# Writing the starting values of two accumulations into the PSUM banks from ScalarE and VectorE, in a kernel of attention and a gated scan

## The chip, the core and the metric

The kernel runs on one core of a Trainium2 chip. A core has five engines with their own instruction queues, each worked in order: PE (TensorE, matrix products, which write only to the accumulator memory PSUM), DVE (VectorE), ACT (ScalarE), POOL (GpSimd) and SP (SyncE, used here to issue DMAs). The scan divides PSUM into 8 banks of 128 partitions by 512 numbers, 2 for y and 6 for all the rest. Weights are loaded into PE by separate instructions (PEld), which overlap products. The metric is the device time of one execution in microseconds (us); lower is better.

## The reference

Two blocks follow each other on x of 8 sequences of 1024 tokens of width 512, each added to x. Everything is float32. The first is a modulated attention with 16 heads; the change does not touch it. The second is a gated state-space scan of inner width 1024 with 16 states:

```
xr, gate = jnp.split(x @ W_in.T, 2, axis=-1)
xr = xr + t_emb[:, None, :]                  # t_emb: the condition, one row per sequence
xc = silu(causal_conv4(xr) + b_conv)
xn = layernorm(xc) * ln_g + ln_b
Bm, Cm, dt = jnp.split(xn @ W_xproj.T, 3, axis=-1)
Ad, Bd = 1.0 + tanh_dt(dt) * A, Bm * minimum(norm(xn), 1.0)
for every token:  h = clip(h * Ad + Bd * xn, -10.0, 10.0);   y_t = sum over states of C * h
y = y + D * xn
return y * silu(gate) @ W_out.T
```

Two sums matter here: the condition added to x @ W_in.T, and D * xn added to y.

## The kernel before

The attention takes the first 3.3 ms, the scan the rest. The scan goes through the 1024 tokens one step at a time, all 8 sequences at once: the state h has 128 partitions (8 sequences x 16 states) by 1024 channels, and a step is one DVE instruction, `step` (L906 to L914, 1.34 us). Before it, `weigh` (L883, ACT) scales the input of that step, which a DMA (`fetch`, L869) has spread over the 128 partitions four steps at a time. After four steps, `products` (L888, PE) multiplies the four states by the masked weights C and adds them in PSUM to y: 8 products of 32 weight columns by 512, which the trace shows as 16 rows. A tile y holds 16 steps; its two banks are one buffer (`ps_y`, L552), so y of the next 16 steps can only begin when the old one has been read.

Around the steps, a chunk of 32 tokens is prepared for the next chunk and finished for the last. The order is written by hand: `at(n, f, ...)` puts a piece of work after step n (L917 to L1003), and every engine gets its instructions in that order. Since all chunks are alike, I give positions 0 to 31 in the repeating chunk: position k is the step k and the pieces placed after it, so `p0 + 51` is position 19. I call the step at position k h(k), and y0 to y7 the eight groups of products of a chunk; group yg is placed at position 4g+4 (y7 at position 0 of the next chunk) and needs h(4g) to h(4g+3).

The pieces that matter:

- `conv_mm` (L638, PE, 8 per chunk, every second position from 21 to 3): four products of x with W_in into a bank, then a fifth (L645) that adds the condition by a product of a 128 x 128 matrix `cond` with repeated columns of the identity. I call them c0 to c7. `conv_in` (ACT) reads the bank, `conv_taps` (DVE) makes the convolution, `conv_out` (ACT) the silu.
- `flip_mm` (L679, PE) turns xs to tokens by channels, `stats`, `center`, `deviation` and `scale` (DVE and ACT) normalise it, `spill` (SP) writes it to DRAM for the fetches, `p_mm` (L670, PE) and `lengths`, `params`, `params_mm`, `params_out`, `spread`, `decay` make the scan's coefficients.
- `fan_mm` (L852, PE) and `fan_out` (L861, ACT, 8 copies of 128 x 512) spread the first four steps of a chunk without a DMA.
- `skip` (L726, DVE) multiplies xt, the normalised tile, by D in place; `add_y` (L807, DVE) adds y from PSUM to it; `gate_y` (L810, DVE) multiplies by the gate. Then `out_flip`, `out_copy`, `out_mm` (PE and ACT) multiply by W_out. `gate_mm` (L792, PE) makes the gate.

Waits that set the order between the engines: h has 6 buffers (`hp`, L547), so h(k) overwrites h(k-6) and waits until the products that read h(k-6) are through: h(2) waits for y7, h(18) for y3. The first group of a tile, y0 or y4, waits until `add_y` has read the tile before. All other banks come from one pool of 6 (`ps_m`, L553).

Of the kernel before, what the change touches and what calls it, by code (L numbers as in the profile page):

```python
# [8 lines left out]
F32 = mybir.dt.float32  # L9
# [6 lines left out]
P = 128  # L16
B = 8
H = 512
KH = H // P
# [503 lines left out]
def gated_scan(ctx, tc, const, tok, x1_d, S, win, tables, w_conv, b_conv, ln_g, ln_b, b_dt, a_log,  # L523
# [44 lines left out]
    x1_now = load_chunk(0)  # L568
    cond_sb = load(cond, "cond", [P, P])
    cw = load(w_conv.rearrange("(k p) j -> p k j", p=P), "cw", [P, KI, 4])  # L570
# [15 lines left out]
    xs_all = tok.tile([P, KI, CW], F32, tag="xq", name="xs")  # L586
    o_sb = tok.tile([P, H], F32, tag="sr", name="o_sb")

    eps = wp.tile([P, 1], F32, name="eps_i")
# [39 lines left out]
    last = {"p": None, "h": None}  # L629

    def load_x1(st, c):
        st["x1"] = load_chunk(c)

    def begin(st):
        nc.scalar.copy(xr[:, :, :, 0:3], xr[:, :, :, TC:])
        st["xs"] = xs_all

    def conv_mm(st, k):  # L638
        ps = st["in", k] = ps_m.tile([P, CW], F32, tag="mm", name="in_ps")
        for kk in range(KH):  # L640
            nc.tensor.matmul(  # L641
                ps, win[kk][:, k * P : (k + 1) * P], st["x1"][:, kk].rearrange("p b t -> p (b t)"),
                start=(kk == 0), stop=False,
            )
        nc.tensor.matmul(  # L645
            ps, cond_sb, ident[:, k * B : (k + 1) * B].unsqueeze(2).to_broadcast([P, B, TC]),
            start=False, stop=True,
        )

# [20 lines left out]
    def p_mm(st):  # L670
        ps = st["pt_ps"] = ps_m.tile([P, NT, P], F32, tag="mm", name="pt_ps")
        for i in range(NT):
            for k in range(KI):
                nc.tensor.matmul(
                    ps[:, i, 0:NX], tile_cols(st["xs"][:, k], i), wx_all[:, k * NX : (k + 1) * NX],
                    start=(k == 0), stop=(k == KI - 1), skip_group_check=True,
                )

    def flip_mm(st, i, half):  # L679
        ps = st["x", i, half] = ps_m.tile([P, 4, P], F32, tag="mm", name="x_ps")  # L680
        for j in range(4):
            nc.tensor.transpose(ps[:, j, :], tile_cols(st["xs"][:, 4 * half + j], i), ident)

# [42 lines left out]
    def skip(st, i):  # L726
        nc.vector.tensor_mul(st["xt", i], st["xt", i], d_bc)

# [14 lines left out]
    def params_mm(st, i):  # L743
        ps = st["xp", i] = ps_m.tile([P, 3, P], F32, tag="mm", name="xp_ps")
        for n in range(3):
            nc.tensor.transpose(ps[:, n], pts[i][:, n * NS : n * NS + P], ident)

# [58 lines left out]

    def add_y(st, i):  # L807
        nc.vector.tensor_add(st["xt", i], st.pop(("y", i)), st["xt", i])  # L808

    def gate_y(st, i):  # L810
        g = st["gate", i]
        nc.vector.tensor_mul(g, st["xt", i], g)

    def out_flip(st, i, half):
        ps = st["gt", i, half] = ps_m.tile([P, 4, P], F32, tag="mm", name="gt_ps")
        for j in range(4):
            k = 4 * half + j
            nc.tensor.transpose(ps[:, j, :], st["gate", i][:, k * P : (k + 1) * P], ident)

# [41 lines left out]
    def fan_out(st, c, half, rs):  # L861
        if half == 0 and rs[0] == 0:
            st["xb"] = xbp.tile([P, 4, DI], F32, name="xb")
            for r in range(4):
                xbs[c * TC + r] = st["xb"][:, r]
        for r in rs:
            nc.scalar.copy(st["xb"][:, r, half * 512 : (half + 1) * 512], st.pop(("fan", r)))  # L867

# [19 lines left out]
    def products(g):  # L888

        c, t = divmod(4 * g, TC)  # L890
        i, q = divmod(t // 4, TT // 4)
        st = sts[c]
        if q == 0:
            st["y", i] = ps_y.tile([P, DI], F32, name="y_ps")
        for hf in range(2):
            for r in range(4):
                nc.tensor.matmul(  # L897
                    st["y", i][32 * r : 32 * r + 32, hf * 512 : (hf + 1) * 512],
                    yws[i][:, 4 * q + r, :],
                    hs[4 * g + r][:, hf * 512 : (hf + 1) * 512],  # L900
                    start=(q == 0), stop=(q == 3), skip_group_check=True,
                )
        for r in range(4):
            del hs[4 * g + r]
# [12 lines left out]
    for c in range(NCH):  # L917
        st, n0 = sts[c], c * TC
        p0 = n0 - TC
        if c > 0:  # L920
            at(p0 + -24 if c > 1 else -34, load_x1, st, c)
        at(p0 + -12, begin, st)
        for k in range(KI):
            at(p0 + -11 + 2 * k, conv_mm, st, k)
            at(p0 + -10 + 2 * k, conv_in, st, k)
            at(p0 + -9 + 2 * k, conv_taps, st, k, (0,))
            at(p0 + -8 + 2 * k, conv_taps, st, k, (1,))
            at(p0 + -7 + 2 * k, conv_taps, st, k, (2,))
            at(p0 + -6 + 2 * k, conv_out, st, k)
        at(p0 + 10, flip_mm, st, 0, 0)  # L930
        at(p0 + 10, flip_mm, st, 0, 1)
        at(p0 + 11, stats, st, 0, 0)
        at(p0 + 11, stats, st, 0, 1)
        at(p0 + 11, center, st, 0)
        at(p0 + 13, deviation, st, 0)
        at(p0 + 14, scale, st, 0)
        at(p0 + 17, spill, st, 0)
        at(p0 + 15, squares, st, 0)
        at(p0 + 27, skip, st, 0)
        at(p0 + 14, flip_mm, st, 1, 0)  # L940
        at(p0 + 14, flip_mm, st, 1, 1)
        at(p0 + 15, stats, st, 1, 0)
        at(p0 + 15, stats, st, 1, 1)
        at(p0 + 15, center, st, 1)
        at(p0 + 16, deviation, st, 1)
        at(p0 + 17, scale, st, 1)
        at(p0 + 24, spill, st, 1)
        at(p0 + 18, squares, st, 1)
        at(p0 + 28, skip, st, 1)
        at(p0 + 21, fan_mm, st, 0)  # L950
        at(p0 + 24, fan_out, st, c, 0, (0, 1))
        at(p0 + 25, fan_out, st, c, 0, (2, 3))
        at(p0 + 26, fan_mm, st, 1)
        at(p0 + 27, fan_out, st, c, 1, (0, 1))
        at(p0 + 28, fan_out, st, c, 1, (2, 3))
        at(p0 + 16, p_mm, st)
        at(p0 + 18, lengths, st)
        at(p0 + 18, params, st, 0)
        at(p0 + 19, params_mm, st, 0)
        at(p0 + 20, params_out, st, 0)  # L960
        at(p0 + 20, params, st, 1)
        at(p0 + 21, params_mm, st, 1)
        at(p0 + 22, params_out, st, 1)
        at(p0 + 22, spread, st)
        at(p0 + 28, decay, st)
        at(p0 + 31, weights, st, 0)
        at(p0 + 46, weights, st, 1)
        at(p0 + 34, order, st, 0)
        at(p0 + 39, gate_mm, st, 0, 0)
        at(p0 + 41, gate, st, 0, 0)  # L970
        at(p0 + 41, gate_mm, st, 0, 1)
        at(p0 + 42, gate, st, 0, 1)
        at(p0 + 51, add_y, st, 0)
        at(p0 + 53, gate_y, st, 0)
        at(p0 + 61, out_flip, st, 0, 0)
        at(p0 + 62, out_copy, st, 0, 0)
        at(p0 + 64, out_mm, st, 0, 0)
        at(p0 + 64, out_flip, st, 0, 1)
        at(p0 + 65, out_copy, st, 0, 1)
        at(p0 + 69, out_mm, st, 0, 1)  # L980
        at(p0 + 71, out_store, st, 0)
        at(p0 + 76, out_send, st, c, 0)
        at(p0 + 49, order, st, 1)
        at(p0 + 50, gate_mm, st, 1, 0)
        at(p0 + 52, gate, st, 1, 0)
        at(p0 + 62, gate_mm, st, 1, 1)
        at(p0 + 67, gate, st, 1, 1)
        at(p0 + 67, add_y, st, 1)
        at(p0 + 72, gate_y, st, 1)
        at(p0 + 75, out_flip, st, 1, 0)  # L990
        at(p0 + 76, out_copy, st, 1, 0)
        at(p0 + 79, out_mm, st, 1, 0)
        at(p0 + 76, out_flip, st, 1, 1)
        at(p0 + 77, out_copy, st, 1, 1)
        at(p0 + 80, out_mm, st, 1, 1)
        at(p0 + 82, out_store, st, 1)
        at(p0 + 90, out_send, st, c, 1)
    for g in range(S // 4):
        if g % (TC // 4) > 0:
            at(4 * g - 9 if g > 2 else -24, fetch, g)  # L1000
        at(4 * g + 4, products, g)
# [14 lines left out]
def network(ctx: ExitStack, tc: tile.TileContext, S, ins, out):  # L1016
# [22 lines left out]
    with tc.manual_schedule():  # L1039
        modulated_attention(  # L1040
            tc, const, xp, tok, x1_d, xu_d, S, ins["x"], ins["xT"], ins["cond"],
            {n: ins[f"w{n}T"] for n in "qkvwu"}, ident, ins["condT"], early, handover,
        )
        gated_scan(
            tc, const, tok, x1_d, S, win, tables, ins["w_conv"], ins["b_conv_c"], ins["ln_g"], ins["ln_b"],
            ins["b_dt"], ins["a_log"], ins["d_skip"], ins["w_out"], ident, ins["cond_k"], ins["mask_y"], ins["sel"], out,
        )
# [70 lines left out]
```

## Time and profile before

| | us |
|---|---|
| median of three runs | 5761.65 (5761.53 to 5765.28) |
| the profiled execution itself | 5764.81 |
| span of its profile | 5763.0 |
| PE busy, of the span | 5582.3 (97%) |
| DVE busy | 4451.3 (77%) |
| ACT busy | 3968.4 (69%) |

The profile comes from one execution. "Busy" is the time in which an engine had an instruction in work; consecutive instructions overlap by some tenths of a microsecond, so the time that one costs in a row of others is the distance from its start to the start of the next, which is less than its duration. "Idle before" is the time that an engine stood still before an instruction, with the engine and line whose end released it; where that line had long been done, it was another. PEclk is the clock that PE was granted, 1.00 being full speed. Lines are those of the kernel before (L...).

The attention ends at about 3338 us. From 3450 us on the scan repeats itself chunk by chunk: y4 starts at 4032.73, 4106.21, 4179.69, 4254.32, 4327.81, 4401.29, 4474.78, 4548.26 us.

### The profile page before, as it was taken

What the parts mean: (1) busy time and instruction counts of PE and PEld (TensorE: products, weight loads), DVE (VectorE), ACT (ScalarE), POOL (GpSimd) and SP (SyncE); (2) the same over time, 40 slices, a digit from 0 to 9 for tenths busy, and PEclk for the clock granted to TensorE, in tenths of its full rate; (3) what the DMA queues carried; (4) which work ended last, traced back from release to release, by engine and by line L of the source; (5) the groups of instructions that cost most, each with busy time, mean ns of one, the idle gap of its engine ahead of it and who ended that gap; (6) DMA issues with size and microseconds to landing.
All of it is one profiled execution on the core that took longest, in us unless ns stands there. A gap on an engine that the chain in (4) does not pass through costs nothing.

```text
span 5763.0 us, 114139 instructions
## 1 busy us (share of the span) xinstructions
PE 5582.3 (97%) x43564; PEld 3242.2 (56%) x43564; DVE 4451.3 (77%) x6930; ACT 3968.4 (69%) x6995; POOL 1541.0 (27%) x1668
## 2 busy tenths in 40 slices
PE   7999999999999999999999989999999999999998
PEld 4656656556556655656566555555555555555553
DVE  4666766766766767667666669999999999999997
ACT  5565655655655655656555568888888888888886
POOL 2433433434434434434333311111111111111111
PEclk9999999999999999999999999999999999999999
DMA  2111212111112112022111268888888888888887
GB/s 83 33 34 54 52 47 62 31 60 51 40 49 67 24 52 72 19 66 55 40 53 31 89 173 230 232 228 229 231 230 228 230 227 230 230 227 229 229 229 189
DMA packets 376962, 714.80 MB, mean 124 GB/s; under 512 B 198176, under 2 KB 280240, under 8 KB 347232
## 3 DMA queue, kind: packets, MB, share of 16 engines
q1 hardware_dynamic: 346416, 684.66, 44.2%
q0 software_dynamic: 30000, 22.83, 1.4%
q8 instruction: 346, 5.67, 0.4%
q14 instruction: 200, 1.64, 0.1%
HBM read 596.58 MB, written 83.89 MB: 118 GB/s over the span
## 4 chain that ended last, share of the span: by engine, by line
PE 62%; DMA 13%; DVE 10%; ACT 9%; SPq 3%; issue 3%; POOL 0%; DVEq 0%; ACTq 0%; POOLq 0%
PE mm_ps L129 17%; PE t_ps L295 14%; PE s_ps L285 9%; DMA xb<-xd 9%; PE t_ps L302 8%; DVE h L910 4%; PE in_ps L641 4%; SPq L876 3%; ACT xb L886 3%; PE y_ps L897 2%; PE o_ps L835 2%; ACT pr L456 2%; PE g_ps L795 1%; DMA bca<-few 1%; DMA x<-x_d 1%
## 5 line engine op out<-in xcount | busy, mean ns | idle before, releaser
L446 DVE TENSOR_REDUCE nmax<-s_ps 128x1 f32<-128x1024 f32 x1024 | 1206.3, 1220 | 460.1 <-PE s_ps L288 459.4
L453 ACT COPY pT<-t_ps 128x512 f32<-128x512 f32 x1024 | 550.7, 589 | 1297.2 <-PE t_ps L295 1296.7
L910 DVE CUSTOM_DVE_ANT_0 h<-h,xb,lim 128x1024 f32<-128x1024 f32 x1024 | 1374.6, 1342 | 81.6 <-ACT x1t L790 26.4
L295 PEld LDWEIGHTS t_ps<-ident,pr 128*128 128x128 f32 x8192 | 911.3, 141 | 659.2 <-issue 490.3
L886 ACT ACTIVATE xb<-xb,ws 128x1024 f32<-128x1024 f32 x1024 | 1157.9, 1163 | 16.9 <-DMA xb<-xd 12.5
L456 ACT ACTIVATE pr<-s_ps,nmax 128x1024 f32<-128x1024 f32 x1024 | 1140.1, 1128 | 1.5 <-DVE nmax L446 1.3
L295 PE MATMUL t_ps<-ident,pr 128*128 128x128 f32 x8192 | 1096.7, 277 | 28.4 <-ACT pT L453 24.7
L475 POOL TENSOR_SCALAR pr<-pr,rinv 128x1024 f32<-128x1024 f32 x512 | 572.5, 1118 | 129.4 <-DVE rinv L474 121.9
L285 PE MATMUL s_ps<-kT,qT 32*128 32x512 f32 x2048 | 596.0, 641 | 2.5 <-ACT pr L456 1.8
L897 PE MATMUL y_ps<-h,yw 128*32 128x512 f32 x4096 | 521.0, 609 | 64.7 <-DVE xt L808 51.7
L288 PE MATMUL s_ps<-k,q 32*128 32x512 f32 x2048 | 578.0, 640 | 1.1 <-DMA q<-qT 1.1
L461 POOL TENSOR_SCALAR pr<-pr,rinv 128x1024 f32<-128x1024 f32 x256 | 286.7, 1120 | 1071.1 <-PE t_ps L295 751.9
L302 PEld LDWEIGHTS t_ps<-pT,vt 128*32 128x32 f32 x16384 | 433.9, 110 | 204.5 <-DVE rinv L469 113.7
L302 PE MATMUL t_ps<-pT,vt 128*32 128x128 f32 x16384 | 506.9, 274 | 16.0 <-DVE pT L467 9.3
L470 POOL TENSOR_SCALAR pr<-pr,rinv 128x1024 f32<-128x1024 f32 x256 | 286.4, 1119 | 841.8 <-DVE rinv L469 792.4
L641 PE MATMUL in_ps<-x,win 128*128 128x256 f32 x2048 | 495.4, 385 | 0.0
L795 PE MATMUL g_ps<-win,x1t 128*128 128x512 f32 x1024 | 467.2, 599 | 1.2 <-ACT x1t L790 1.2
L835 PE MATMUL o_ps<-wout,xt 128*128 128x512 f32 x1024 | 459.0, 596 | 0.0
L641 PEld LDWEIGHTS in_ps<-x,win 128*128 128x128 f32 x2048 | 378.3, 191 | 133.4 <-ACT xb L867 49.4
L847 POOL DMA_DIRECT2D out<-o_sb x256 | 150.9, 595 | 1038.1 <-ACT o_sb L841 965.5
L758 POOL DMA_DIRECT2D bca<-few x256 | 129.1, 513 | 1094.8 <-ACT few L751 1056.3
L467 DVE COPY pT<-t_ps 128x512 f32<-128x512 f32 x512 | 352.0, 688 | 54.3 <-PE t_ps L295 54.1
(149 smaller groups left out, 7181.0 us busy)
## 6 DMA issues: line engine op xcount, KB each, us to landing
xb<-xd SPq DMA_DIRECT2D x1792, 256.0 KB
xd<-xt SPq DMA_DIRECT2D x64, 512.0 KB
q<-qT SPq DMA_DIRECT2D x128, 128.0 KB
xr<-in_xT SPq DMA_DIRECT2D x64, 256.0 KB
xu_d<-xr SPq DMA_DIRECT2D x64, 256.0 KB
xr<-xu_d SPq DMA_DIRECT2D x64, 256.0 KB
x_d<-xr SPq DMA_DIRECT2D x64, 256.0 KB
out<-o_sb POOLq DMA_DIRECT2D x256, 64.0 KB, 5.5
```

What stands on the lines that cost most here:

```text
L129: nc.tensor.matmul(ps, w, x, start=(k == 0), stop=(k == KH - 1))
L285: nc.tensor.matmul(s_ps[i][:, 0:HW], st["q"][r, qc], st["k"][r, 0:HW], start=True, stop=True)
L288: nc.tensor.matmul(s_ps[i][:, HW:S], st["q2"][r, qc], st["k2"][r], start=True, stop=True)
L295: nc.tensor.transpose(ps[:, j], pr[:, c0 : c0 + P], ident)
L302: nc.tensor.matmul(av[r], vt[:, kt, r], pT[:, i, kt], start=(kt == 0), stop=(kt == KT - 1), skip_group_check=True,)
L446: nc.vector.tensor_reduce(nmax[i], s_ps[i], AX.X, ALU.max, negate=True)
L456: nc.scalar.activation(fresh[i], s_ps[i], AF.Exp, bias=nmax[i], accum_out=rsum[i])
L641: nc.tensor.matmul(ps, win[kk][:, k * P : (k + 1) * P], st["x1"][:, kk].rearrange("p b t -> p (b t)"), start=(kk == 0), stop=False,)
L835: nc.tensor.matmul(ps, st["gT", i][:, k, :], wout_sb[:, k, :], start=False, stop=(k == KI - 1), skip_group_check=True,)
L886: nc.scalar.mul(xbs[n], xbs[n], sts[c]["ws"][:, t : t + 1])
L897: nc.tensor.matmul(st["y", i][32 * r : 32 * r + 32, hf * 512 : (hf + 1) * 512], yws[i][:, 4 * q + r, :], hs[4 * g + r][:, hf * 512 : (hf + ...
L910: nc.vector._custom_dve(dve_ops.TENSOR_ADD_SAT, out=h, in0=last["h"], in1=xbs.pop(n), s0=lim[:, 0, t : t + 1], s1=lim[:, 1, t : t + 1],)
```

## The change

1. `conv_mm` loses the fifth product. Two positions earlier a new piece `conv_open` (ACT) writes the condition into the bank by a copy from SBUF to PSUM, and the four products add to it.
2. `skip` takes a y tile and writes D * xn into its two banks (DVE, SBUF to PSUM); all products of that tile add to it. `add_y` is gone, and `gate_y` reads y from PSUM.
3. Of the 8 copies of `fan_out`, 4 go to DVE.
4. At the start of the scan 8 more products write all banks once, with `start` set. Later the flips and `p_mm` set `start` on the first product of a bank only, and the products of `conv_mm` and `products` not at all; `p_mm` gets one more product (128 x 160 zeros) for the columns that its others leave out.
5. Many pieces move by some positions. `skip` goes from positions 27 and 28 to 3 (first tile, right after `gate_y` of the tile before) and 20 (second tile, after `gate_y` at 19 and the step h(20)). The second `params` moves from 20 to 19, `params_mm` of it from 21 to 20, the flips of the first tile from 10 to 9, `gate_mm` of the first tile's second half from 9 to 11, the load of x for the chunk after next from 8 to 15.

```diff
-    cond_sb = load(cond, "cond", [P, P])
+    cT = load(cond.rearrange("(k p) b -> p k b", p=P), "cT", [P, KI, B])
...
+    for _ in range(6):
+        ps = ps_m.tile([P, CW], F32, tag="mm", name="any_ps")
+        nc.tensor.matmul(ps, ident, ident[:, 0:1].to_broadcast([P, CW]), start=True, stop=True)
+    ps = ps_y.tile([P, DI], F32, name="y_ps")
+    for hf in range(2):
+        nc.tensor.matmul(
+            ps[:, hf * 512 : (hf + 1) * 512], ident, ident[:, 0:1].to_broadcast([P, 512]), start=True, stop=True
+        )
...
+    def flip(ps, x, start, stop):
+        nc.tensor.matmul(ps, x, ident, start=start, stop=stop, is_transpose=True, skip_group_check=True)
...
+    def conv_open(st, k):
+        ps = st["in", k] = ps_m.tile([P, CW], F32, tag="mm", name="in_ps")
+        nc.scalar.copy(ps.rearrange("p (b t) -> p b t", b=B), cT[:, k].unsqueeze(2).to_broadcast([P, B, TC]))
+
     def conv_mm(st, k):
-        ps = st["in", k] = ps_m.tile([P, CW], F32, tag="mm", name="in_ps")
+        ps = st["in", k]
         for kk in range(KH):
             nc.tensor.matmul(
                 ps, win[kk][:, k * P : (k + 1) * P], st["x1"][:, kk].rearrange("p b t -> p (b t)"),
-                start=(kk == 0), stop=False,
-            )
-        nc.tensor.matmul(
-            ps, cond_sb, ident[:, k * B : (k + 1) * B].unsqueeze(2).to_broadcast([P, B, TC]),
-            start=False, stop=True,
-        )
+                start=False, stop=(kk == KH - 1), skip_group_check=True,
+            )
...
+        nc.tensor.matmul(
+            ps[:, :, NX:], ident, zero[:, 0:1].unsqueeze(2).to_broadcast([P, NT, P - NX]),
+            start=False, stop=True, skip_group_check=True,
+        )
...
     def skip(st, i):
-        nc.vector.tensor_mul(st["xt", i], st["xt", i], d_bc)
+        y = st["y", i] = ps_y.tile([P, DI], F32, name="y_ps")
+        nc.vector.tensor_mul(y, st["xt", i], d_bc)
...
-    def add_y(st, i):
-        nc.vector.tensor_add(st["xt", i], st.pop(("y", i)), st["xt", i])
-
     def gate_y(st, i):
         g = st["gate", i]
-        nc.vector.tensor_mul(g, st["xt", i], g)
+        nc.vector.tensor_mul(g, st.pop(("y", i)), g)
...
-            nc.scalar.copy(st["xb"][:, r, half * 512 : (half + 1) * 512], st.pop(("fan", r)))
+            (nc.scalar.copy, nc.vector.tensor_copy)[r % 2](st["xb"][:, r, half * 512 : (half + 1) * 512], st.pop(("fan", r)))
...
-        at(p0 + -12, begin, st)
+        at(p0 + -14, begin, st)
         for k in range(KI):
+            at(p0 + -13 + 2 * k, conv_open, st, k)
...
-        at(p0 + 10, flip_mm, st, 0, 0)
-        at(p0 + 10, flip_mm, st, 0, 1)
+        at(p0 + 9, flip_mm, st, 0, 0)
+        at(p0 + 9, flip_mm, st, 0, 1)
...
-        at(p0 + 27, skip, st, 0)
+        at(p0 + 35, skip, st, 0)
...
-        at(p0 + 28, skip, st, 1)
+        at(p0 + 52, skip, st, 1)
...
-        at(p0 + 20, params, st, 1)
-        at(p0 + 21, params_mm, st, 1)
+        at(p0 + 19, params, st, 1)
+        at(p0 + 20, params_mm, st, 1)
...
-        at(p0 + 51, add_y, st, 0)
-        at(p0 + 53, gate_y, st, 0)
+        at(p0 + 51, gate_y, st, 0)
...
-        at(p0 + 67, add_y, st, 1)
-        at(p0 + 72, gate_y, st, 1)
+        at(p0 + 67, gate_y, st, 1)
```

## The prediction

> **What bounds the kernel now.** I read the page's 40 slices first: from 3.4 ms on PE and DVE are both at nine tenths, so the scan, where the whole edit lies, has two rivals for its bound. Next a table by windows (columns: PE, weight loads, DVE, ACT, POOL, granted PE clock, DMA share, GB/s):
>
> ```profile
> 4000.00:4500.00 500.00, 489.79 (x2488) 267.36 (x2487) 473.81 (x685) 435.26 (x754) 61.23 (x112) 1.00 0.86 230
> 4242.40:4245.80 3.40, 3.40 (x35) 3.35 (x36) 3.23 (x8) 3.10 (x7) 0.00 (x0) 1.00 1.05 260
> 4245.90:4249.30 3.40, 3.40 (x17) 0.47 (x12) 2.26 (x2) 2.06 (x5) 0.00 (x0) 0.50 0.93 231
> 3399.40:3402.70 3.30, 1.08 (x3) 0.17 (x4) 3.09 (x4) 3.30 (x7) 0.00 (x0) 1.00 0.00 0
> 3402.80:3406.20 3.40, 3.20 (x4) 0.18 (x3) 3.40 (x5) 3.40 (x10) 0.00 (x0) 0.50 0.00 0
> ```
>
> PE is busy 98% of a stretch of seven chunks, DVE 95%, ACT 87%; DMA at 0.86 has room. Rows two to five matter later: after a window in which PE ran only `p_mm`'s 48-column products, or three short ones, 3.4 us at clock 0.50 follow.
>
> Then the timeline of one chunk on PE (start, duration, and in brackets the idle time before):
>
> ```profile
> 4106.21 1.92 PE L897 MATMUL y_ps<-h,yw 128*32 128x512 f32 x16 [1.53 <-DVE xt L808]
> ...
> 4136.07 1.92 PE L897 MATMUL y_ps<-h,yw 128*32 128x512 f32 x16
> 4137.93 1.99 PE L641 MATMUL in_ps<-x,win 128*128 128x256 f32 x8
> ...
> 4172.28 1.93 PE L897 MATMUL y_ps<-h,yw 128*32 128x512 f32 x16
> 4174.13 3.70 PE L795 MATMUL g_ps<-win,x1t 128*128 128x512 f32 x8
> 4177.67 0.49 PE L746 MATMUL xp_ps<-ident,pt 128*128 128x128 f32 x3
> 4179.69 1.92 PE L897 MATMUL y_ps<-h,yw 128*32 128x512 f32 x16 [1.53 <-DVE xt L808]
> ```
>
> These are y4, y7, y3 and the next y4: 73.48 us a chunk, with one hole, in which y4 waits for `add_y`. DVE's timeline says why that comes when it does:
>
> ```profile
> 4138.11 1.34 DVE L910 CUSTOM_DVE_ANT_0 h<-h,xb,lim 128x1024 f32<-128x1024 f32 x1 [1.03 <-ACT x1t L790]
> ...
> 4157.39 1.29 DVE L687 BATCH_NORM_STATS2 stat<-x_ps 128x6 f32<-128x512 f32 x2 [0.68 <-PE x_ps L682]
> ...
> 4177.17 1.34 DVE L910 CUSTOM_DVE_ANT_0 h<-h,xb,lim 128x1024 f32<-128x1024 f32 x1
> 4178.43 1.22 DVE L808 TENSOR_TENSOR xt<-y_ps,xt 128x1024 f32<-128x1024 f32 x1
> ```
>
> DVE gets slack back twice: h(2) waits for the buffer that y7 reads (y7 is through at 4137.93, 0.18 earlier; the engine named had long been done), and `stats` waits for the flips. From 4157.39 on it has no further wait before `add_y`. So the present cycle is: y4 to the first `stats` on PE without a hole, 51.18; `stats` to the next y4 on DVE, 22.30. Period 73.48; with four half-clock chunks (about 1.15 each over some 30, 0.15 a chunk) 73.63.
>
> **The change part by part.** Prices are distances from start to start in these timelines; durations stand in the groups of 3400 to 5600 us, and on the page for the last row:
>
> ```profile
> L645 PE MATMUL in_ps<-ident,cond 128*128 128x256 f32 x472 | 140.4, 379 | 0.0
> L727 DVE TENSOR_TENSOR xt<-xt,d_bc 128x1024 f32<-128x1024 f32 x60 | 73.2, 1220 | 2.8 <-DMA xd<-xt 2.6
> L808 DVE TENSOR_TENSOR xt<-y_ps,xt 128x1024 f32<-128x1024 f32 x59 | 71.9, 1219 | 0.0
> L867 ACT COPY xb<-fan_ps 128x512 f32<-128x512 f32 x240 | 133.0, 632 | 0.0
> L467 DVE COPY pT<-t_ps 128x512 f32<-128x512 f32 x512 | 352.0, 688 | 54.3 <-PE t_ps L295 54.1
> ```
>
> *PE.* Per chunk 8 products of L645 go, 0.43 each (4111.25 to 4111.68): -3.46. The zero product comes, between 160/256 of that, 0.27, and all of it, 0.43; I take 0.27. PE's work falls from 71.95 (73.48 less the hole of 1.53) to 68.8.
>
> *DVE.* Two `add_y` (1.13) go; `skip` stays two, now into PSUM. No row has DVE write a wide tile to PSUM; L727 and L808, reading SBUF and PSUM, both take 1.22, so I take no difference, with 0.3 each way. Four fan copies come: L467's neighbours start 0.60 apart, duration 0.69 as the upper end; 2.4 a chunk. Sum -2.3 + 2.4: DVE's work is unchanged, about 72.3 us a chunk as worked out below.
>
> *ACT.* 8 `conv_open` come. The nearest row is the copy of 128 x 256 by L652, from PSUM (402 ns, 0.26 apart when in a row); no row has that copy write PSUM, but L721 writes it at 592 ns for 512 columns, no more than L867's 632, so 0.26 to 0.40, and I take 0.26: +2.1. Four fan copies go (0.47 apart): -1.9. ACT stays near 64 of 73; nothing behind it on the queue is more than 0.2 later, and `weigh` runs two steps ahead.
>
> *SP and POOL.* The loads of x, spills and fetches move by one to seven positions past each other; with DMA share 0.86 and no wait on a fetch in the chain here I cost them at nothing. If that cover is gone a late fetch holds `weigh` and h.
>
> *The order.* This decides. The old cycle relaxes: 51.18 loses 3.46, the second flip of params (0.38, now before y4) and the gate's product of 3.45 now behind the flips, and gains two flips of the output ahead (1.0): 44.9. The DVE half, 22.30, loses `weights` (0.41, now at position 9) and gains what now stands before y4, `params` of the second tile (0.75), h(20) (1.255) and `skip` (1.14): 25.0. Together 69.9.
>
> But y4 no longer waits for `add_y`, early at position 19: it waits for `skip`, behind `gate_y`, `params` and h(20). So the second cycle, y4 to y7 on PE, h(2), DVE to `skip`, y4, becomes the longest:
> - PE, y4 to y7's end: 31.72 (4106.21 to 4137.93) - 0.38 - 6 x 0.43 = 28.76
> - to h(2): 0.18
> - DVE, h(2) to the end of what y4 waits for: 41.45 (4138.11 to 4179.56), less the waits in it 0.84 (0.68 and 0.16 at the deviation), + 3.15 as above, + 0.5 (two more pairs without a small instruction between: h directly after h starts 1.51 apart against 1.255), = 44.26
> - to y4: 0.13.
>
> Sum 73.33. DVE's own remainder, from `skip` to h(2), is 32.04 (4179.56 to the next chunk's h(2)) - 1.47 (its waits) - 2.0 (h(20) and `params`, moved ahead of y4) - 3.4 (`gate_y` and the two old `skip`) + 2.4 + 0.5 (two more such pairs of h) = 28.0, against 29.07 on PE with the two hand-overs: so DVE alone would need 72.3, and h(2) still waits 1.0 for y7. The 3.2 saved on PE do not shorten the chunk: PE gives them back at y4.
>
> *The hole.* y3 must end before `gate_y` at position 19. From y3's end to y4 DVE does h(18), the rest of position 18, h(19), `gate_y`, `params`, h(20), `skip`: about 8.95. PE has in that time the gate's 3.45 and six short flips. The hole grows from 1.53 to a stretch of 5.5 with 0.8 of work in it. The clock rows above say what that risks: 3.4 us windows on a fixed grid, and half clock in the window after one with little PE work. A stretch of 3.5 (`p_mm`) was caught 4 times in 31 chunks; on a grid of 3.41 that is a tolerance of 0.35. So 5.5 is caught with (5.5 + 0.35 - 3.41)/3.41 = 0.72, and what is left of the half-clock window after y4 has begun is 1.0 to 3.4 us, costing half, 0.5 to 1.7, mean 1.1. It falls on y4 to y7, in the longest cycle: 0.8 a chunk, from 0 to 1.7.
>
> [...]
>
> *Ends.* Per chunk 73.33 + 0.15 + 0.8 = 74.28 against 73.63: +0.65, times 30 chunks +19. Before the loop, eight small products (0.43 at most each) and 8 x 0.43 less: nothing. The last chain loses an `add_y`: -1.3. The last chunk is DMA-paced in the trace (DMA share 1.00 to 1.05) and gains less: I take -2. So +16 on the profiled 5764.8 = 5781; the median is 3.2 below that execution: 5777.
>
> **Rivals.**
> 1. *The clock holds* (the flips count as enough work, or the hole is shorter): 73.48, -0.15 x 30 - 1.3 = -6: 5756, no change. For it: the hole of 1.53 was never caught. Against: the gap at 3397.4 to 3401.0, 3.6 us, was.
> 2. *Other side: DVE alone decides.* If PE from y4 to y7 is 1.0 shorter than I have it, or the hand-over at position 20 that much earlier, h(2) no longer waits and the period is DVE's 72.3 + 0.15: -1.2 x 30 = -36: 5725. Price per 0.1: 3 us; from 0.3 on it is measurable. It needs a clock that holds at least in most chunks.
> 3. *Dearer writes.* `skip` into PSUM at 0.3 more, twice in the longest cycle's DVE part, and the full 1.7 in every chunk: 73.33 + 0.6 + 1.7: +2.0 x 30 = +60; either alone +34 to +45: 5796 to 5822.
> 4. *The engines' writes do not seed the sum:* the same instructions, the same time. Nothing in the profile can show it, and it has no price. [...]
>
> **How the numbers follow.** Likeliest, half clock in most chunks: 0.50, 5765 to 5797. Rival 1: 0.20, 5750 to 5765. Rival 2: 0.18, 5718 to 5750. Rival 3: 0.12, above 5797. A measurement can tell about 0.2%, 11.5 us, so faster is below 5750, slower above 5773. Faster: rival 2 and a part of rival 1 (caught chunks that still gain), 0.26. Slower: rival 3 and four fifths of the likeliest, 0.52. Same: 0.22. For 8 in 10 I leave out 0.1 below 5732 and 0.1 above 5805.
>
> **What would show it.** After the change: no L645; y4's wait on DVE's `skip` in every chunk, 4 to 5 us of PE idle around the flips of params; granted clock 0.50 in the window after it in some seven chunks of ten; h(2) waiting 1 us and more for y7; no wait at `stats`; periods between 73.3 and 75.0. Wrong if the period is below 73 with h(2) not waiting (rival 2), if the clock stays at 1.00 (rival 1), or if DVE's copies, `skip` or ACT's `conv_open` show durations above 0.69, 1.22 and 0.40.

## The result, and the profile after

The changed kernel takes 5810.95 us (5808.68 to 5812.49) against 5761.59 us: a ratio of 1.0083, interval 1.0071 to 1.0095. It is 49 us slower; I had forecast 15.

The table by windows of the changed kernel has the same stretch as before and the surroundings of one y4 (PE, weight loads, DVE, ACT, POOL, granted PE clock, DMA share, GB/s):

```profile
4000.00:4500.00 500.00, 470.32 (x2344) 244.98 (x2342) 466.32 (x686) 429.67 (x762) 54.91 (x100) 0.98 0.86 227
4121.60:4126.30 4.70, 0.53 (x4) 0.31 (x3) 4.43 (x7) 4.67 (x9) 0.00 (x0) 1.00 0.97 287
4126.30:4129.70 3.40, 3.06 (x16) 0.69 (x16) 1.44 (x2) 2.16 (x6) 2.30 (x5) 0.51 1.00 313
4129.70:4133.10 3.40, 3.40 (x21) 1.83 (x17) 2.69 (x2) 0.99 (x3) 1.76 (x4) 0.99 0.54 155
```

PE fell from 489.79 to 470.32 us of 500, DVE from 473.81 to 466.32, ACT from 435.26 to 429.67: no engine is fuller, and the same work takes longer. The second row is the hole before y4, with 0.53 us of work in 4.7; the third is one window of 3.4 us at half clock.

PE's timeline of the changed kernel: y3, the gate's products, the flips of params, y4 (half clock), y7, and the next y4.

```profile
4115.73 1.92 PE L914 MATMUL y_ps<-h,yw 128*32 128x512 f32 x16
4117.58 3.70 PE L817 MATMUL g_ps<-win,x1t 128*128 128x512 f32 x8
4121.12 0.49 PE L645 MATMUL xp_ps<-ident,pt 128*128 128x128 f32 x3
4123.95 0.52 PE L645 MATMUL xp_ps<-ident,pt 128*128 128x128 f32 x3 [2.34 <-DVE pt L763]
4126.64 3.46 PE L914 MATMUL y_ps<-h,yw 128*32 128x512 f32 x16 [2.17 <-DVE y_ps L749]
4130.03 1.99 PE L661 MATMUL in_ps<-x,win 128*128 128x256 f32 x8
...
4155.21 1.92 PE L914 MATMUL y_ps<-h,yw 128*32 128x512 f32 x16
4157.06 3.72 PE L661 MATMUL in_ps<-x,win 128*128 128x256 f32 x16
...
4201.73 3.46 PE L914 MATMUL y_ps<-h,yw 128*32 128x512 f32 x16 [2.17 <-DVE y_ps L749]
```

And DVE's: h(20), `skip`, h(22) waiting for y4, h(2) waiting for y7 (4157.06, 0.18 earlier; the engine named had long been done).

```profile
4124.00 1.34 DVE L927 CUSTOM_DVE_ANT_0 h<-h,xb,lim 128x1024 f32<-128x1024 f32 x1 [0.20 <-DMA xb<-xd]
4125.27 1.23 DVE L749 TENSOR_TENSOR y_ps<-xt,d_bc 128x1024 f32<-128x1024 f32 x1
...
4130.20 1.34 DVE L927 CUSTOM_DVE_ANT_0 h<-h,xb,lim 128x1024 f32<-128x1024 f32 x1 [2.46 <-PE y_ps L914]
...
4157.24 1.34 DVE L927 CUSTOM_DVE_ANT_0 h<-h,xb,lim 128x1024 f32<-128x1024 f32 x1 [0.80 <-ACT xb L905]
```

The idle before y4 grew from 1.53 to 2.34 + 2.17, `stats` waits no longer, and h(2) waits 0.80 for y7 (1.03 before; I had forecast 1.0). The rest of this was forecast too. What was not: y4 takes 3.39 to its next instruction instead of 1.85, and not in seven chunks of ten but in every one. The period is 75.09 where I had 74.28. Here it repeats to 0.01 us (y4 at 4126.64, 4201.73, 4276.81, 4351.89); over thirty chunks it lies between 74.89 and 75.45.

The trace's record of the granted clock shows where that number comes from. Half clock comes in stretches, or windows, of 3.413 us. From 3529 to 5703 us they follow each other at 75.09 us, one at every y4, with 71.68 us of full clock between them, which is 21 times 3.413. So 75.09 is 22 windows: 75.09 / 22 = 3.413. The windows lie on a fixed grid: in this trace, and in that of the kernel before, every change of the granted clock lies within 0.01 us of a whole number of 3.4133 us behind the first. Between the four windows that the kernel before has in its steady chunks the clock is full for 365.23, 512.00 and 365.23 us, 107, 150 and 107 windows.

Where the 47.6 us between the two profiled executions (5810.6 and 5763.0) lie: y4 starts first at 3450.06 against 3442.61, +7.5; thirty chunks of 75.117 against 73.718 on average, +42.0; from the 31st y4 to the end, the last chunk included, 107.0 against 108.8, -1.8.

### The profile page after: what moved, and what is told of

Same layout as the page of the kernel before. It is cut to its first block, busy times and chain, and to the rows that moved or that the text cites. A ratio compares the mean times of both kernels' runs of the same rounds, so it can differ in the third digit from the quotient of the medians.

```text
span 5810.6 us, 113475 instructions
## 1 busy us (share of the span) xinstructions
PE 5525.5 (95%) x43132; PEld 3162.8 (54%) x43132; DVE 4456.1 (77%) x6994; ACT 3979.9 (68%) x7123; POOL 1542.4 (27%) x1668
## 4 chain that ended last, share of the span: by engine, by line
PE 67%; DMA 12%; DVE 10%; ACT 7%; SPq 2%; issue 2%; DVEq 0%; POOL 0%; ACTq 0%; POOLq 0%
PE mm_ps L129 17%; PE t_ps L295 14%; DMA xb<-xd 9%; PE s_ps L285 9%; PE t_ps L302 8%; PE in_ps L661 5%; PE y_ps L914 4%; DVE h L927 4%; PE o_ps L854 3%; PE g_ps L817 2%; SPq L895 2%; ACT pr L456 2%; ACT xb L905 1%; DMA x<-x_d 1%; ACT pT L453 1%
## 5 line engine op out<-in xcount | busy, mean ns | idle before, releaser
L446 DVE TENSOR_REDUCE nmax<-s_ps 128x1 f32<-128x1024 f32 x1024 | 1206.3, 1220 | 461.1 <-PE s_ps L288 460.4
L905 ACT ACTIVATE xb<-xb,ws 128x1024 f32<-128x1024 f32 x1024 | 1170.4, 1163 | 63.0 <-DMA xb<-xd 45.5
L914 PE MATMUL y_ps<-h,yw 128*32 128x512 f32 x4096 | 553.7, 651 | 80.6 <-DVE y_ps L749 76.7
L661 PE MATMUL in_ps<-x,win 128*128 128x256 f32 x2048 | 482.3, 386 | 15.8 <-ACT in_ps L656 15.8
```

The costliest lines, as they stand in the source:

```text
L446: nc.vector.tensor_reduce(nmax[i], s_ps[i], AX.X, ALU.max, negate=True)
L661: nc.tensor.matmul(ps, win[kk][:, k * P : (k + 1) * P], st["x1"][:, kk].rearrange("p b t -> p (b t)"), start=False, stop=(kk == KH - 1), s ...
L905: nc.scalar.mul(xbs[n], xbs[n], sts[c]["ws"][:, t : t + 1])
L914: nc.tensor.matmul(st["y", i][32 * r : 32 * r + 32, hf * 512 : (hf + 1) * 512], yws[i][:, 4 * q + r, :], hs[4 * g + r][:, hf * 512 : (hf + ...
```

## Experiments: is it the clock?

The theory: in each chunk y4 meets what is left of a half-clock window. If y4 comes later in it, less is left, and the loss is smaller; so the chunk settles where its own path and the loss together make a whole number of windows. The path without loss would be 75.09 - 1.54 = 73.55, and the rest is the clock. The changed kernel's own trace supports this: one y4 comes 0.35 later than usual (4577.59, idle 2.52 before it), and the four chunks after it take 74.89, 74.99, 75.04 and 75.06. Their distance to 75.09 halves each time, as it must if a later arrival in the half-clock window gets half of its delay back.

**Filling the hole.** The fillers stand behind the three flips of each `params_mm`, 14 in the first run and 8 in the second; the block that they write is read by nobody:

```diff
-        ps = st["xp", i] = ps_m.tile([P, 3, P], F32, tag="mm", name="xp_ps")
+        ps = st["xp", i] = ps_m.tile([P, 4, P], F32, tag="mm", name="xp_ps")
         for n in range(3):
             flip(ps[:, n], pts[i][:, n * NS : n * NS + P], n == 0, n == 3 - 1)
+        for n in range(14):
+            nc.tensor.matmul(ps[:, 3], ident, ident, start=False, stop=True, skip_group_check=True)
```

> The changed kernel with 14 idle products (128 x 128, into a column block that nobody reads) behind the flips of each params, in the hole of PE before y4; nothing else is changed. Theory 1 (the chunk is locked to the clock's grid: 75.09 us = 22 windows of 3.413, y4 takes 1.54 more at half clock; without it the path y4, y7, h(2), skip is 73.55): clock 1.00 throughout, y4 1.85 to its next instruction, period 73.5 to 73.7, 30 x 1.5 = 45 us less than the changed kernel: 5763 to 5770. Rival (the half clock falls into slack, the period is set by the hand-over alone): stays at 5808 to 5815, clock 1.00 or not.

5821.47 us, ratio 1.0102 (1.0087 to 1.0117): outside both. The clock did hold at every y4 (its mean over the profiled execution is 0.994, against 0.985 in the changed kernel), but each filler is two instructions of 0.11, so 14 took 3.1 us in holes of 2.3 and 2.2, and y4 came about as much later as the half clock had cost: the period is 75.03. The time above the changed kernel lies before the first y4, which starts at 3460.63 instead of 3450.06.

> As the run with 14 filler products, but 8. There each filler product showed as two instructions of 0.11, so 14 took 3.1 us where the holes are 2.3 and 2.2 long, and y4 came 1.6 later than it need have: the lost clock was won back and spent on the filler. 8 take 1.8 and fit. Theory 1: no half-clock window at y4, y4 not delayed, period 73.55 (y4 to y7 28.9, h(2) to skip 44.4, hand-overs 0.3) instead of 75.09: 5811 - 47 = 5764, range 5758 to 5770. Rival (the period does not follow the clock): 5805 or more.

5779.07 us, ratio 1.0031 (1.0020 to 1.0042), 32 us less than the changed kernel. Its timeline, with y4 at full clock and one chunk of 73.52:

```profile
4188.42 1.95 PE L770 MATMUL xp_ps<-ident 128*128 128x128 f32 x16
4190.91 0.52 PE L645 MATMUL xp_ps<-ident,pt 128*128 128x128 f32 x3 [0.54 <-DVE pt L763]
4191.27 1.95 PE L770 MATMUL xp_ps<-ident 128*128 128x128 f32 x16
4193.60 1.92 PE L916 MATMUL y_ps<-h,yw 128*32 128x512 f32 x16 [0.38 <-DVE y_ps L749]
...
4267.12 1.92 PE L916 MATMUL y_ps<-h,yw 128*32 128x512 f32 x16 [0.38 <-DVE y_ps L749]
```

Most chunks take 73.53, as the theory had it to 0.02. The time missed its range by 9 us: the first y4 comes 6.8 later than in the changed kernel, and eight of thirty chunks take 74.7 to 75.1. In the clock record these eight have a half-clock window behind `p_mm`, as four chunks of the kernel before had it. All but one of the intervals between them are 221.9 us, three chunks or 65 windows: off the first lock, the chunks fall into another.

**Adding work.** Memsets of a scratch tile on DVE right before the `skip` that y4 waits for: two of 128 x 256 as below (lag05), one of 128 x 256 (lag03), one of 128 x 128 (lag02).

```diff
+        for _ in range(2 if i == 1 else 0):
+            nc.vector.memset(late, 0.0)
         y = st["y", i] = ps_y.tile([P, DI], F32, name="y_ps")
```

> The changed kernel with 0.5 us more on DVE (two memsets of 128 x 256 of a scratch tile) right before the skip that y4 waits for. Theory 1 (locked to the grid): y4 starts 0.5 later in its half-clock window, so it loses only about 1.0 instead of 1.54; period stays 75.09, time 5808 to 5816. Rival (no lock, a loss that does not depend on the arrival): the 0.5 adds in full, period 75.6, +15 us: 5823 to 5829.

5846.12 us, ratio 1.0146 (1.0131 to 1.0161): 35 us more, worse than either expected. y4's idle is 0.64 longer than in the changed kernel, and the clock now stays down for two windows (6.8 us) in two of three chunks. Where a second window followed, the first had at most 2.42 us of busy PE; where none followed, at least 2.69. Three chunks (76.99, 76.05, 75.64) repeat; their sum, 228.68, is 67 windows of 3.413.

> The changed kernel with one memset of 128 x 128 on DVE before the skip that y4 waits for, about 0.2 (two of 128 x 256 held y4 back by 0.64). Theory 1 (lock, with one half-clock window): y4 comes 0.2 later in its window and loses 1.34 instead of 1.54; period stays 75.09, time 5808 to 5816 although a chunk has more work. Rival (no lock: the loss is 1.54 whatever the arrival, or 75.09 = 22 x 3.413 is chance): 30 x 0.2 = 6 more and above, 5815 to 5825, period 75.3.

> The same with one memset of 128 x 256, about 0.35. Theory 1: loss 1.2, period 75.09, 5808 to 5816, as long as the window that y4 starts in keeps enough work behind y4 (2.4 of its 3.4 us) not to bring a second half-clock window, as it did with 0.64 (two windows, 6.8 us, in two of three chunks). Rival: 30 x 0.35 = 10 more and above, 5819 to 5830, period 75.4 or more.

5814.95 us, ratio 1.0094 (1.0080 to 1.0108), within the theory's range, and 5820.88 us, 1.0103 (1.0089 to 1.0117), within the rival's. The memsets cost 0.12 and 0.25 at y4. Four y4 of the first, then four of the second, from their timelines of PE:

```profile
4050.40 3.34 PE L917 MATMUL y_ps<-h,yw 128*32 128x512 f32 x16 [2.29 <-DVE y_ps L752]
4125.48 3.35 PE L917 MATMUL y_ps<-h,yw 128*32 128x512 f32 x16 [2.29 <-DVE y_ps L752]
4200.57 3.35 PE L917 MATMUL y_ps<-h,yw 128*32 128x512 f32 x16 [2.29 <-DVE y_ps L752]
4275.67 3.35 PE L917 MATMUL y_ps<-h,yw 128*32 128x512 f32 x16 [2.29 <-DVE y_ps L752]
```

```profile
5033.98 3.23 PE L917 MATMUL y_ps<-h,yw 128*32 128x512 f32 x16 [2.42 <-DVE y_ps L752]
5109.08 3.23 PE L917 MATMUL y_ps<-h,yw 128*32 128x512 f32 x16 [2.42 <-DVE y_ps L752]
5184.17 3.23 PE L917 MATMUL y_ps<-h,yw 128*32 128x512 f32 x16 [2.42 <-DVE y_ps L752]
5259.27 3.23 PE L917 MATMUL y_ps<-h,yw 128*32 128x512 f32 x16 [2.42 <-DVE y_ps L752]
```

This is the lock: with 0, 0.12 and 0.25 more in the path, y4 takes 3.46, 3.35 and 3.23, and the period stays 75.09 to 75.10. In the clock record y4 begins about 0.26, 0.48 and 0.72 into its half-clock window: it moves by about twice the added work, because half clock gives back half of a delay. In lag03 the time still rose, because the lock has an edge. In the three runs with memsets a second window followed where y4 began 0.83 or more into the first, and nowhere else. lag03 settles close to that: three times it fell for two to three chunks into double windows (76.6) and took several more to come back. So the period is locked, and added work is free only as long as nothing disturbs it.

| kernel | chunks that repeat | sum | in windows of 3.413 |
|---|---|---|---|
| changed; lag02 and lag03 while settled | 75.09 | 75.09 | 22 |
| lag05 | 76.99, 76.05, 75.64 | 228.68 | 67 |
| cond_pe (below) | 78.16, 78.84 | 157.00 | 46 |
| early (below) | 73.27, 74.51, 73.63, 72.13 | 293.54 | 86 |

## Experiments: which part of the change costs?

**The condition back on PE, in the changed order**: the fifth product of L645 restored, `conv_open` gone.

> The changed kernel with the condition back on PE (fifth product, no conv_open); y seeds, fan copies and positions stay. The path y4, y7, h(2), skip, y4 gets 6 products of 0.43 back: 73.55 + 2.58 = 76.1 without clock loss. Theory 1: the next multiple of the window, 78.5, would need a loss of 2.4, over what a window can cost, so no lock; 0 to 1.7 a chunk, mean 0.8: period about 76.9, 30 x 3.2 = 96 over the kernel before, the start back to that of before, end -2: 5835 to 5880. Rival (the seeds of y cost little, and the clock is all): 73.7 + 0.8 a chunk or less, at most 5790.

5906.45 us, ratio 1.0251 (1.0236 to 1.0266), beyond the range: I had reckoned with single windows only. From the sixth chunk on every second one has a double window, and two chunks lock to 46 windows; 78.5 is reached after all, with 2.4 lost a chunk. The direction stands: without the products saved, the rest of the change (y seeds, fan copies and positions together) costs 144 us, about half of it (30 x 2.4) by the clock. What the y seeds cost by themselves this run does not separate.

**The condition alone, in the old order**: from the kernel before, `conv_open` at `p0 + -12 + 2 * k`, the fifth product gone, whole banks written by the flips and `p_mm`.

> The kernel before with the condition alone changed: conv_open by ScalarE one position ahead of its four products, the fifth product gone, the flips and p_mm writing whole banks; skip, add_y, fan copies and all other positions as before. My cycles: y4-flips-stats-y4 73.48 - 3.46 = 70.0; y4-y7-h(2)-y4 72.64 - 2.58 = 70.1; DVE alone 73.48 less its waits of 1.0 + 0.7 + 0.2 + 0.3 = 71.3. Theory (the condition's move is a gain that the y seeds eat up): DVE decides, period 71.3 to 71.8, 30 x 2.1 = 63 us less, start up to 7 more as in the changed kernel: 5695 to 5710. Rival (PE's slack lands in the hole before y4 and is caught by the clock, or conv_open makes ACT late): 5735 or more.

5883.37 us, ratio 1.0213 (1.0196 to 1.0230): the rival. The groups of 3460 to 5560 us show why (busy, mean ns, idle before):

```profile
L652 PE MATMUL in_ps<-x,win 128*128 128x256 f32 x1760 | 441.1, 395 | 152.2 <-ACT in_ps L647 152.2
```

One position ahead is too late: PE waits 152.2 us for `conv_open`, and the period is 76.80. In the changed kernel, two positions ahead, the same group waits 2.4 us (3400 to 5600 us). So this run tells nothing of what the condition is worth, but what its new wait costs where ACT's queue is not given time.

**Without the y seeds, in the changed order**: `skip` in place at positions 27 and 28, `add_y` at 19 and 3 as before, products that start their banks. Once with all fan copies on ACT, once with half on DVE as changed.

```diff
-        y = st["y", i] = ps_y.tile([P, DI], F32, name="y_ps")
-        nc.vector.tensor_mul(y, st["xt", i], d_bc)
+        nc.vector.tensor_mul(st["xt", i], st["xt", i], d_bc)
...
+        at(p0 + 51, add_y, st, 0)
+        at(p0 + 53, gate_y, st, 0)
```

> The changed kernel without the y seeds and with all fan copies on ACT: skip in place at 27 and 28 and add_y at 51 and 67 as before, products start their banks; conv_open two positions ahead of its products and every other position as changed. Paths: y4, y7, h(2), add_y, y4: 28.9 + 0.2 + 40.6 + 0.1 = 69.8; DVE alone about 71.3, so a half-clock loss of 1.5 at y4 is free. Theory (the condition by ScalarE is a gain once conv_open comes early enough): period 71.3 to 72.0, 30 x 2 = 60 less than the kernel before, start 7 more: 5700 to 5722. Rival (ACT, with 2.1 a chunk more, makes weigh or conv_open late): 5750 or more, with waits of h on xb.

> The changed kernel without the y seeds (skip in place at 27 and 28, add_y at 51 and 67, products start their banks), fan copies as changed, half on DVE. DVE alone needs the 72.13 of the early skip and two add_y of 1.13: 74.4; the path y4, y7, h(2), add_y has 69.8, so a half-clock loss at y4 is free. Theory: DVE decides, period 74.4 to 74.7, 30 x 0.8 more than the kernel before and 7 at the start: 5789, range 5780 to 5800; then the y seeds are worth 2.3 a chunk on DVE, and cost more than that through the order they were put in. Rival (the y seeds as such are what makes the changed kernel slow): 5765 or less.

5800.75 us (ratio 1.0068, 1.0053 to 1.0083) and 5806.65 us (1.0074, 1.0061 to 1.0088). The first went the rival's way: h stands 56.8 us behind `weigh`, and PE's `out_flip` behind the fan copies. In the second, DVE decides as expected, 74.5 to 74.7 in undisturbed chunks (where it never waits more than 0.40), but I missed the range by 7 us, since half-clock windows still add to some chunks (mean 74.97). The first line is of the first, the second of the second:

```profile
L645 PE MATMUL gt_ps<-ident,gate 128*128 128x128 f32 x452 | 71.0, 280 | 35.7 <-ACT xb L888 35.7
```

```profile
L645 PE MATMUL gt_ps<-ident,gate 128*128 128x128 f32 x448 | 70.5, 280 | 52.3 <-DVE xb L888 52.3
```

So taking the seeds away does not give the old time back. Whichever engine makes the fan copies, `out_flip` now waits behind them (35.7 and 52.3 us in the lines above), presumably for a bank, which no run shows; in the changed kernel this group has no wait.

## Experiments: mending the order

**`skip` earlier.** y4 waits for `skip` behind `params` and h(20). Neither has to be there:

```diff
         at(p0 + 51, gate_y, st, 0)
+        at(p0 + 51, skip, st, 1)
...
-        at(p0 + 52, skip, st, 1)
...
-        at(p0 + 19, params, st, 1)
-        at(p0 + 20, params_mm, st, 1)
+        at(p0 + 20, params, st, 1)
+        at(p0 + 21, params_mm, st, 1)
```

> The changed kernel with skip of the second tile right behind gate_y (position 19 instead of 20), params of the second tile behind it (20), its flips at 21. y4 then waits neither for params (0.75) nor for h(20) (1.26). Theory (the hand-over at position 20 is what the y seeds cost, directly and through the clock): the path y4, y7, h(2), skip falls from 73.55 to 71.5, so DVE decides (72.3 to 72.8), and the hole is about 2 shorter and rarely caught: 5811 - 30 x 2.5 = 5736, range 5722 to 5748. Rival (another wait takes its place: params_out, spread and decay come one position later, or y4 still meets a half-clock window): 5765 or more.

> The kernel of the run with the early skip, with all fan copies on ACT again. DVE loses 2.4 a chunk: alone 69.9; the path y4, y7, h(2), skip is 71.5 and decides: period 71.5 to 72.2, 5811 - 30 x 3.3 = 5711, range 5698 to 5725. Rival (the fan copies were moved for ACT's sake: ACT, with 1.9 a chunk more, makes weigh late): no better than the early skip alone, or slower.

5756.24 us, ratio 0.9992 (0.9982 to 1.0001), and with all fan copies on ACT 5821.07 us, 1.0102 (1.0085 to 1.0119). The early skip takes 55 us off the changed kernel, but I missed the range by 8: a chunk without half clock takes 72.13, as expected, and three of four are not. Four y4 in turn:

```profile
4253.00 2.80 PE L914 MATMUL y_ps<-h,yw 128*32 128x512 f32 x16 [2.85 <-DVE y_ps L749]
4326.27 3.25 PE L914 MATMUL y_ps<-h,yw 128*32 128x512 f32 x16 [2.83 <-DVE y_ps L749]
4400.78 3.54 PE L914 MATMUL y_ps<-h,yw 128*32 128x512 f32 x16 [2.38 <-DVE y_ps L749]
4474.42 1.92 PE L914 MATMUL y_ps<-h,yw 128*32 128x512 f32 x16 [2.85 <-DVE y_ps L749]
```

The shorter hole is caught as often as a lock of 86 windows over four chunks has it. The fan copies on ACT are the rival's case again: h waits 88.8 us for `weigh`, and the period is 75.47 on average. That wait is not all of it: in the clock record y4 meets a half-clock window in every chunk, and settled chunks take 75.10, again 22 windows. What the copies cost by themselves the run does not say.

**Real work in the hole.** The first `conv_mm` of the next chunk, 1.73 of products, one position earlier, ahead of y4:

```diff
-            at(p0 + -11 + 2 * k, conv_mm, st, k)
+            at(p0 + (-11 + 2 * k if k else -12), conv_mm, st, k)
```

> The changed kernel with one piece moved by one position: the first conv_mm of the next chunk (four products, 1.73) from 21 to 20, so that it stands before y4 and not behind it. It fills the second half of the hole with real work and leaves the path from y4 to y7. That path falls from 73.53 (the clean chunk of the run with 8 filler products) to 71.8; the next longest is y4, h(22), DVE, skip, y4: 75.09 - 1.54 - 0.80 = 72.75. Theory (the loss is the clock's, and goes with the length of the low stretch, 5.5 before, about 2.9 now): no half clock at y4, some at p_mm (0.2 a chunk): period 72.95, 5811 - 30 x 2.17 = 5746, range 5736 to 5756. Rival (y4 is only pushed back, as by the 14 filler products, or the half clock stays): 5775 or more.

> The early skip and the early conv_mm together. With the early skip alone a chunk without half clock took 72.13, with DVE never waiting, but four chunks in turn took 73.27, 74.51, 73.63 and 72.13. Theory: with 1.73 of the 2.85 idle before y4 filled, only p_mm's stretch is caught (0.2 to 0.4 a chunk): period 72.4, 5756 - 30 x 0.96 = 5727, range 5718 to 5738, faster than both kernels. Rival (DVE's floor is not 72.13 once PE's order changes, or half clock stays): 5745 or more.

Alone it gives 5772.74 us, ratio 1.0016 (1.0007 to 1.0025), 38 us better than the changed kernel but 17 beyond its range: a clean chunk takes 73.06, and 19 half-clock windows still come in thirty chunks, in the other half of the hole (2.34 between the flips of the two tiles) or behind `p_mm`. With the early skip: **5723.85 us, ratio 0.9931 (0.9918 to 0.9943)**, within its range and 40 us faster than the kernel before. Three y4 of it:

```profile
4174.95 1.92 PE L914 MATMUL y_ps<-h,yw 128*32 128x512 f32 x16 [0.72 <-DVE y_ps L749]
4247.11 1.92 PE L914 MATMUL y_ps<-h,yw 128*32 128x512 f32 x16 [0.73 <-DVE y_ps L749]
4319.25 1.92 PE L914 MATMUL y_ps<-h,yw 128*32 128x512 f32 x16 [0.72 <-DVE y_ps L749]
```

The hole is down to 0.72, y4 is never at half clock, 26 of 30 chunks take 72.0 to 72.2, and four take 73.3, with a half-clock window behind `p_mm`.

**`p_mm` in two**: the products of its first tile before y3, the rest behind it, `gate_mm` one position later.

> As the run before it, with p_mm cut in two: the 16 products of the first tile before y3, those of the second and the zero product behind it, the gate's products one position later. No stretch of low PE work is then as long as a window of 3.41. Theory: every chunk takes DVE's 72.13: 5756 - 30 x 1.2 = 5719, range 5711 to 5728. Rival (the half clock does not come from p_mm, or the cut delays params): no faster than the run before it.

5723.53 us, ratio 0.9930 (0.9917 to 0.9944): the four chunks are gone, and from 4000 to 4760 us the granted clock never falls, so those windows did come from `p_mm`. But a chunk now takes 72.22, 0.07 more, so the mean falls only from 72.30 to 72.25. I had expected the gain without the price.

**What the condition is worth.** The version of 5723.85 us with the fifth product back and no `conv_open`:

> The version with the early skip and the early first conv_mm (72.15 in a chunk without half clock, DVE never waiting), with the condition by PE's fifth product again. It asks what the condition by ScalarE is worth once the order is mended. Path y4, y7, h(2), skip: 28.88 - 1.73 + 0.38 + 5 x 0.43 = 29.7, + 0.3 + 42.35 = 72.35; PE has 68.8 + 3.5 = 72.3 of work. Theory (the condition on ScalarE gives room on PE, not time, where DVE needs 72.15): period 72.4 to 73.2, 5724 + 8 to 5724 + 32 less 5 at the start: 5727 to 5751, still faster than the kernel before. Rival (PE's room is what the order lives on): 5762 or more.

5753.60 us, ratio 0.9988 (0.9979 to 0.9997): 30 us more than with the condition on ScalarE, 3 beyond the range. The chunk is 73.39 in all but two, y4 waits only 0.22, and PE leaves no other gap: PE's own work, 73.2 where I had 72.3, decides. I had called the condition's move room, not time; it is worth 1.24 a chunk once the room is not lost again.

**The start.** The first four `conv_open` of the second chunk ahead of the first `decay`, which holds ACT until a DMA has landed (8.92 us of waiting in the changed kernel):

```diff
-            at(p0 + -13 + 2 * k, conv_open, st, k)
+            at(-21 if c == 1 and k < 4 else p0 + -13 + 2 * k, conv_open, st, k)
```

> The same version with the first four conv_open of the second chunk moved ahead of the decay of the first, which holds ACT until a DMA lands. In the changed kernel PE stood still for 11.6 us there, where PE worked on that chunk's products before; the first y4 came 7.5 later. Theory (the wait that the change adds on ACT's queue costs that start): PE's products of k = 0 to 3 lie in the wait, h(0) comes about 4 us earlier, 5724 - 4 = 5720, range 5716 to 5722. Rival (the start hangs on the DMA and the decay alone): 5723 to 5726.

5719.52 us, ratio 0.9930 (0.9917 to 0.9944), 4.3 less than without it; the ranges of the two overlap, so the traces have to decide. First the changed kernel, in which PE stands 11.62 us behind `conv_open` (10.81 in the version without the move), then this one:

```profile
3389.17 8.80 PE L661 MATMUL in_ps<-x,win 128*128 128x256 f32 x32 [11.62 <-ACT in_ps L656]
```

```profile
3375.18 7.17 PE L661 MATMUL in_ps<-x,win 128*128 128x256 f32 x32 [0.19 <-ACT in_ps L656]
```

The first 32 products now lie in the wait; PE waits 8.83 behind the fifth `conv_open` instead. From ACT's table load behind that DMA to h(0) it is 10.4 us in the kernel before (3389.18 to 3399.61), 16.0 in the changed one (3386.94 to 3402.92), 17.0 in the version without the move (3388.60 to 3405.62), and 12.2 here (3384.35 to 3396.53). So by these two traces the move takes 4.8 off the start, near the 4 expected.

## Why the prediction was wrong

**Right: the hand-over.** "y4 no longer waits for `add_y` ...: it waits for `skip`" holds, and so does the sum of the second cycle, 73.33. Measured without the clock: y4 to y7's end 4157.06 - 4126.64 - 1.54 = 28.88 (I had 28.76), h(2) to the next y4 44.49 (44.39), in all 73.55; and 73.53 in the run with 8 fillers. DVE's own need, forecast as 72.3, is 72.15 in the mended order, where it never waits more than 0.33 in a chunk without half clock. The hole, forecast at 5.5, ran from 4121.1 to 4126.6.

**Wrong: the term "0.8 a chunk".** This is the step that failed: the loss at y4 was seen, but mis-sized. I took the grid to fall at random on the hole, a chance of 0.72 times a mean of 1.1. But the loss sets when the next hole comes, so the phase is not free: a y4 early in the half window loses more and comes relatively later next time (begun 0.26, 0.48 and 0.72 into it, y4 took 3.46, 3.35 and 3.23). It settles at the loss that fills the path up to 22 windows, 1.54, in every chunk: 0.74 a chunk more than I had, 22 us. The path's 0.22 gave 7 more, and `p_mm`'s 0.15, which the lock keeps out, took 4 back; that the kernel before was 0.09 a chunk slower than my 73.63 took another 3. With 7.5 at the start and 1.5 less gained at the end than I had, that makes 31 of the 32 between 47.6 and the forecast 16.

**Wrong: "Before the loop ...: nothing".** I counted the instructions and not the queue. `conv_open` stands on ACT behind `decay`, and PE behind `conv_open`. The first y4 comes 7.5 us later. From the table load behind the DMA to h(0) the changed kernel takes 5.6 longer, and from h(0) to y4 4.1 longer (47.1 against 43.0); the load itself came 2.2 earlier. What the 4.1 is made of stays open. My working followed the queues through the steady chunk and left out the first.

The full loss of 1.7 a chunk, half of a window, was nearer to 1.54 than my mean was. That was luck: 1.54 is what fills the path up to 22 windows, and half of a window is 1.7 whatever the path. The upper end of the range, 5805, took the dearer writes and the full loss as alternatives to the likeliest case; the start was in none of them.

The rivals: the clock did not hold; the engines' writes to PSUM were not dear (`skip` 1230 ns against 1220, `conv_open` 415 against a bound of 400; neither comes near 49 us); DVE alone decides only in the mended order; and whether the writes seed the sum cannot be read from a time.

## What to carry to other kernels

Here the work taken off one engine turned into waiting at the next hand-over, so look for what the waiter now waits for and move that first; one `skip` (with `params` behind it) and one product group moved by one position turned a loss of 0.8% into a gain of 0.7%. A periodic kernel with a stretch of little PE work in each period need not meet the clock's grid at random (here 75.09 us was 22 windows of 3.413): look whether the period is a whole number of windows, and distrust small experiments while it is. When a wait is added to a queue, follow it through the first round of the loop as well as through the steady one.

## What was not expected of the hardware

- A chunk of 73.53 us runs as one of 75.09 = 22 x 3.413 us, and 0.12 or 0.25 us of added work shorten the half-clock loss by the same 0.11 and 0.23.
- In lag05 half clock lasted two windows, 6.8 us, in two of three chunks: there the first window held at most 2.42 us of busy PE, against 2.69 or more where one window was all.
- The fill of the hole had to fit: 3.1 us of fillers cost as much as the 1.54 us of half clock that they saved (period 75.03 against 75.09); 1.73 us of work that had to be done anyway cost 0.02 (a chunk without half clock takes 72.15, against 72.13 with the early skip alone).
- ScalarE's and VectorE's writes into PSUM take about what the nearest rows took: 415 ns for 128 x 256 (402 for a copy from PSUM to SBUF), 1230 ns for 128 x 1024 (1220 to SBUF).
